# Context keys of a Perceiver layer: turned on VectorE and through DRAM instead of on TensorE; weight sums placed behind the first layer norm

## The chip, the cores and the metric

One core of one Trainium2 chip. The metric is the time of one execution on the device in microseconds (us), median of three runs. All data and all matmuls are float32.

## The reference, cut to what matters

One layer on 256 latent tokens `x` (width 512) with a context of 4096 tokens: cross attention, then a Mamba block, then a mixture of experts, each behind a layer norm. The change is in the attention:

```python
h = layernorm(x)                                    # (256, 512)
q = rope(rms_norm(h @ wq, q_norm_w))                # 16 heads of 128
k = rope(rms_norm(h @ wk, k_norm_w)); v = h @ wv    # 4 key-value heads of 128
kc = rms_norm(ctx @ wk_ctx, k_norm_w)               # context: 4096 keys, no rope
vc = ctx @ wv_ctx
scores = q @ concat(kc, k).T / sqrt(128) + mask     # context open, own tokens causal
out = softmax(scores) @ concat(vc, v) @ wo
x = x + out                                         # then Mamba, then the experts
```

`rms_norm(y, w)` is `y * rsqrt(mean(y*y) + eps) * w`. For a context key this is one factor per key and head, and a weight vector `w` over the 128 channels; the query sees the weights only through the product of the two.

## The kernel before, in words

The program is written with one instruction stream per engine (TensorE is PE, VectorE is DVE, ScalarE is ACT, GpSimd is POOL, SyncE is SP and issues most DMAs). Each engine works through its own stream in order. A scheduler places the instructions of all steps into the streams by their dependencies; semaphore waits follow from the tiles.

**Bounded arm.** A flag computed from the norm weights selects between two arms of the program (L1339). In the arm that runs (`bounded`), no running maximum is kept: the exponent is shifted by a constant.

**Prologue** (L416 to L463). Layer norm of the two token tiles (`layernorm`, L187; its power is a POOL instruction, `power_half`, L181). Then come key and value products of context chunk 0 (`context_pieces`, L273), key, value and query products of the own tokens (`self_block`, L429, ten of these), and for each of the ten a norm and rope in `norm_rope` (L401): ACT copies the product (L404) and squares it (L242), DVE does the rope (L409 to L412) and prepares the power (L184), POOL raises it (`r`, L185) and multiplies (`lacc`, L413), and PE turns the block by four 128x128 transposes (`selfT`, L437).

**Weight sums** (`fast_weights`, L297). The other seven chunks of 512 context tokens use a Strassen-like scheme of seven products for eight. It needs four sums of quarters of `wkv` (the context weights of keys and values in one tile), all on POOL: T1, T2 and T4 (L305 to L307) into weight buffers that come free late in the prologue, and T3 in place (L308). Sums of a context chunk, S1 to S4 (L320 to L323), are POOL's too.

**Attention** (`bounded_attention`, L496). Stage s (0 to 8) scores one chunk of keys: stage 0 the own keys in 12 steps, stage s the context chunk s-1 in 32 steps (4 groups of heads, 2 token tiles, 4 key tiles). A step is a score product (`scT`, L512), an exponential on ACT (L515, its scale `rk` carries the key's norm factor), a running sum on DVE (L523) and, two steps later, a value product (`oT`, L532). From stage 2 on key tiles are taken in the order 1, 3, 2, 0 (`keys_of`, L492).

**Beside the steps** of stages 1 to 7 the next chunk's keys and values are made (`fast_steps`, L310): `extra` is a list of closures, called one by one between the steps at L568. There are 14 products (`ps_kv`, L328), whose results DVE and ACT add up into `kraw` (keys, tokens on partitions) and `v`; after the sixth and the seventh of each half, `key_rms` (L245) squares a key tile for its norm factor. Four `key_transpose` (L265) are among the extras: four PE transposes of 128x128 (`kTp`, L269), then an ACT copy times the key norm weights into `kT` (L270), which lies with channels on partitions. The last two extras load a context chunk and clear a piece of the experts' gather buffer in DRAM.

**Tiles.** `krp` has two buffers of tag `sq`, for the squares. `kvp` has two `kT` and two `v`. `wpool` has six weight buffers; `oacc` and `lacc` are large accumulators, used as scratch in the prologue.

Of the kernel before, what the change touches and what calls it, by code (L numbers as in the profile page):

```python
# [19 lines left out]
P = 128  # L20
# [47 lines left out]
def perceiver_layer(ctx: ExitStack, tc: tile.TileContext, a: dict, out: bass.AP):  # L68
# [17 lines left out]


    load_ctx0 = lambda i, n: nc.sync.dma_start(ctx0[:, i:i + n], a["ctxT"][0, :, i:i + n])
    load_ctx0(0, 1)
    for k in range(0, KD, 2):  # L90
        nc.sync.dma_start(wkc[:, k:k + 2, :], a["wk_ctx"][k * P:(k + 2) * P, :].rearrange("(k p) n -> p k n", p=P))
    nc.sync.dma_start(x_sb, a["x"].rearrange("(t p) d -> p t d", p=P))
    load_ctx0(1, 1)
    load_ctx0(2, 2)
# [21 lines left out]
    xg = tc.dram_tile((ROUNDS * NE * P, DM), FP, name="xg")  # L116
    ye = tc.dram_tile(((NE + 1) * P, DM), FP, name="ye")
    ye2 = tc.dram_tile(((NE + 1) * P, DM), FP, name="ye2")
    sums_d = [tc.dram_tile((SH, P), FP, name=f"sums{t}") for t in range(NT)]

    rope = const.tile([P, NT, 2, HALF], FP, name="rope")
# [7 lines left out]
    def layer(ctx, bounded):  # L129
# [51 lines left out]
        def power_half(dst, src, scale, eps, n):  # L181

            v = small.tile([P, NH], FP, tag="pv", name="pv")
            V.tensor_scalar(v[:, :n], src, scale, eps, ALU.mult, ALU.add)  # L184
            G.tensor_tensor(dst, v[:, :n], mhalf[:, :n], ALU.pow)  # L185

        def layernorm(t):  # L187

            st = small.tile([P, 6], FP, tag="bn", name="bn")
            V.bn_stats(st, x_sb[:, t, :])  # L190
            mv = small.tile([P, 2], FP, tag="mv", name="mv")
            V.bn_aggr(mv, st)
            rs = small.tile([P, 1], FP, tag="rs", name="rs")
            power_half(rs, mv[:, 1:2], 1.0, 1e-5, 1)
            V.tensor_scalar(xn[:, t, :], x_sb[:, t, :], mv[:, 0:1], rs, ALU.subtract, ALU.mult)

        def turn_xn(t, tp):

# [58 lines left out]
        def context_tiles(c):  # L257

            kT = kvp.tile([P, NKV, CK], FP, tag="kT", name="kT")
            v = kvp.tile([P, CK // P, NKV * HD], FP, tag="v", name="v")  # L260
            r = small.tile([P, CK // P, NKV], FP, tag="rk", name="rk", bufs=2)
            kv[c + 1] = (kT, v, r)
            raws = {}

            def key_transpose(i):  # L265
                tp = ps_tp.tile([P, NKV, P], FP, tag="tp", name="kTp")
                raw = raws.pop(i)
                for h in range(NKV):
                    TE.transpose(tp[:, h, :], raw[:, h, :], ident)  # L269
                S.activation(kT[:, :, i * P:(i + 1) * P], tp, AF.Copy, scale=kw_col)  # L270
            return v, r, raws, key_transpose

        def context_pieces(c):  # L273

            ct = ctx_tiles.pop(c)
            v, r, raws, key_transpose = context_tiles(c)

            def key_piece(i):
                ps = ps_mm.tile([P, 512], FP, tag="mm", name="ps_k")
                project(ps, lambda k: ct[:, i, k, :], lambda k: wkc[:, k, :])  # L280
                raws[i] = raw = krp.tile([P, NKV, HD], FP, tag="kraw" if i == 1 else "kn", name="kraw")
                S.copy(raw, ps.rearrange("p (h d) -> p h d", d=HD))
                key_rms(raw, r[:, i, :])

            def value_piece(i):
                ps = ps_mm.tile([P, 512], FP, tag="mm", name="ps_v")
                project(ps, lambda k: ct[:, i, k, :], lambda k: wvc[:, k, :])
                S.copy(v[:, i, :], ps)

            return [[lambda i=i, f=f: f(i) for i in range(CK // P)] for f in (key_piece, value_piece, key_transpose)]  # L290
# [3 lines left out]

        fast = {}

        def fast_weights():  # L297
            fw = [wpool.tile([P, KD, 512], FP, tag="w", name=f"fast{i}") for i in range(3)]
            T = (2, 2, 256)
            fast["T2"], fast["T4"] = carve(fw[0], T, T)  # L300
            fast["S2"], fast["S4"], fast["u3"], fast["u2"] = carve(fw[1], (2, 2, P), (2, 2, P), (2, 256), (2, 256))

            fast["T1"], fast["S1"], fast["S3"] = carve(fw[2], T, (2, 2, P), (2, 2, P))
            b11, b12, b21, b22 = (wkv[:, :, k:k + 2, n:n + 256] for k in (0, 2) for n in (0, 256))
            G.tensor_tensor(fast["T1"], b12, b11, ALU.subtract)  # L305
            G.tensor_tensor(fast["T2"], b22, fast["T1"], ALU.subtract)
            G.tensor_tensor(fast["T4"], b21, fast["T2"], ALU.subtract)  # L307
            G.tensor_tensor(b12, b22, b12, ALU.subtract)  # L308

        def fast_steps(c):  # L310
            ct = ctx_tiles.pop(c)
            v, r, raws, key_transpose = context_tiles(c)
            T1, T2, T4, S1, S2, S3, S4, u3, u2 = (fast[n] for n in ("T1", "T2", "T4", "S1", "S2", "S3", "S4", "u3", "u2"))
            wide = lambda n: (lambda k: wkv[:, :, n % 2 * 2 + k, n // 2 * 256:n // 2 * 256 + 256])
            w11, w21, T3, w22 = (wide(n) for n in range(4))
# [14 lines left out]
            def row(j):  # L330

                m = {}
                bank = lambda: ps_mm.tile([P, 2, 256], FP, tag="mm", name="ps_kv")
                here = lambda i, k0: (lambda k: ct[:, i, k0 + k, :])
                part = lambda s: (lambda k: s[:, j, k, :])

                def put(i, h, ps, more=None):

                    if i not in raws:
                        raws[i] = krp.tile([P, NKV, HD], FP, tag="kraw" if i < 2 else "kn", name="kraw")  # L340
                    to = (raws[i].rearrange("p h d -> p (h d)")[:, h * 256:h * 256 + 256], v[:, i, h * 256:h * 256 + 256])
                    for n in range(2):
                        if more is None:
                            S.copy(to[n], ps[:, n, :])
                        else:
                            V.tensor_tensor(to[n], ps[:, n, :], more[:, n, :], ALU.add)  # L346

                def p1():
                    m["x"] = bank()
                    product(m["x"], here(j, 0), w11)  # L350
                    S.copy(u3, m["x"])

                def p6():
                    m["y"] = bank()
                    product(m["y"], part(S2), by(T2))
                    V.tensor_tensor(u2, m["y"], u3, ALU.add)

                def p2():
                    product(m["x"], here(j, 2), w21, False)
                    put(j, 0, m["x"])  # L360

                def p7():
                    product(m["y"], part(S3), T3, False)
                    V.tensor_tensor(u3, m["y"], u3, ALU.add)

                def p5():
                    m["z"] = bank()
                    product(m["z"], part(S1), by(T1))
                    put(j + 2, 1, m["z"], u3)

                def p4():
                    product(m["y"], here(j + 2, 2), by(T4))
                    put(j + 2, 0, m["y"], u3)
                    key_rms(raws[j + 2], r[:, j + 2, :])

                def p3():
                    product(m["z"], part(S4), w22, False)
                    put(j, 1, m["z"], u2)
                    key_rms(raws[j], r[:, j, :])
                return [p1, p6, p2, p7, p5, p4, p3]  # L380

            turn = lambda i: (lambda: key_transpose(i))
            first, then = row(1), row(0)
            sums()
            return first + then[0:2] + [turn(3)] + then[2:3] + [turn(1)] + then[3:] + [turn(2), turn(0)]


        tab_q, tab_k = carve(oacc, (2, NT, HD), (2, NT, HD))
        room = carve(lacc, *[(REP, HD)] * 8)

        take_ro, take_ru = ring([room[i] for i in (0, 1, 4, 5, 7)]), ring([room[i] for i in (2, 6, 3)])
# [26 lines left out]
        kv[0] = (kT0, v0, None)  # L418
        ctx_k, ctx_v, ctx_t = context_pieces(0)
        for t in range(NT):  # L420
            layernorm(t)
        for i in range(3):
            ctx_k[i]()
        for t in range(NT):
            turn_xn(t, ps_sc.tile([P, 512], FP, tag="sc", name="lnT"))
        rope_table(tab_k, kw_bc)
        rope_table(tab_q, qw_bc)

        def self_block(t, w, tb, dst):  # L429
            ps = ps_mm.tile([P, 512], FP, tag="mm", name="ps_self")  # L430
# [49 lines left out]


        wo = [wpiece(a["wo"][j * 512:(j + 1) * 512, :], f"wo{j}") for j in range(3)]
        fast_weights()
        w_x = []

        def last_weights():
# [9 lines left out]
        def bounded_attention(beside):  # L496
# [50 lines left out]
            for s in range(NC + 1):  # L547
# [4 lines left out]
                    last_weights()  # L552
                extra = []
                if 0 < s < NC:
                    extra = fast_steps(s)
                    if s + 1 < NC:
                        extra.append(lambda: load_ctx(s + 1))
                    extra.append(lambda: clear(s - 1))
                done = 0
                for n, st in enumerate(steps):  # L560
                    if s == 0 and n == 3:
                        for turn in turns:
                            turn()
                    pending.append((*st, scores(*st)))
                    if len(pending) > 2:
                        values(*pending.pop(0))
                    if s < NC:
                        while done < len(extra) * (n + 1) // len(steps):  # L568
                            extra[done]()
                            done += 1  # L570
                    elif n > len(steps) // NT + 1:
# [823 lines left out]
```

## Time and profile before

| | |
|---|---|
| median of 3 runs | 1034.38 us (1034.35 to 1034.86) |
| the profiled execution: its time | 1035.15 us |
| its span, first to last instruction | 1033.4 us |
| granted TensorE clock, mean | 0.997 |
| chain that ended last | PE 91%, POOL 2%, DMA 2%, DVE 2%, ACT 1% of the span |
| prologue, stages 0 to 8, rest | to about 89 us, to about 760 us, to the end |
| `kTp` transposes, L269 | 128, in 32 groups of 4 |
| `kT` copies, L270 | 32, mean 688 ns |

Times in the profile are microseconds from the span's start, or ns where it says "mean ns". A row of groups has line, engine, operation, output and inputs by the program's names, shapes and count; then busy time and mean of one; then the engine's idle time just before, and what ended it. PEld is TensorE's loading of the stationary operand. Each float32 matmul appears as two passes ("x2"). Matmul ends are modelled, since matmuls overlap in a pipeline, so the rate is read from starts: one pass of 128x512 starts 0.43 us after the other.

### The profile page before, as it was taken

The numbers are of one execution on the slowest core, as the hardware profiler recorded it, in microseconds if no ns is written. First come the engines' busy times: TensorE is split into PE (matmuls) and PEld (weight loads), VectorE is DVE, ScalarE is ACT, GpSimd is POOL, SyncE is SP. The second block draws the span as 40 slices with busy tenths as digits, with TensorE's granted clock in tenths as the row PEclk, the third lists the DMA queues.
The fourth block names the chain that finished last, engine by engine and source line by source line (L and its number), as shares of the span: only waits on it lengthen the run. The fifth ranks groups of instructions, "written<-read, shape, count | busy, mean of one in ns | idle before, by whom it ended". The sixth has DMA issues, their size and how long they took to land.

```text
span 1033.4 us, 9074 instructions
## 1 busy us (share of the span) xinstructions
PE 1009.6 (98%) x2930; PEld 492.4 (48%) x2930; DVE 476.7 (46%) x947; ACT 397.1 (38%) x887; POOL 157.2 (15%) x156
## 2 busy tenths in 40 slices
PE   7998999999999999999999999999999999999997
PEld 3443444444444444444444444444556555555553
DVE  2346544344444443443543534466786563322133
ACT  3544344434444534434434434442353531222210
POOL 2374002001001100200200200000023322000022
PEclk9999999999999999999999999999999999999999
DMA  9997001000000100100100000300153457999833
GB/s 336 380 406 273 0 1 41 1 0 22 20 1 1 41 0 1 41 0 1 41 0 1 22 0 1 122 1 0 44 203 122 154 214 285 369 363 360 302 111 97
DMA packets 41499, 113.05 MB, mean 109 GB/s; under 512 B 3777, under 2 KB 4706, under 8 KB 40290
## 3 DMA queue, kind: packets, MB, share of 16 engines
q1 hardware_dynamic: 34336, 96.83, 26.0%
q0 software_dynamic: 2208, 8.39, 2.3%
q10 hardware_dynamic: 4898, 7.16, 1.9%
q8 instruction: 25, 0.41, 0.2%
q14 instruction: 32, 0.26, 0.1%
HBM read 81.42 MB, written 30.95 MB: 109 GB/s over the span
## 4 chain that ended last, share of the span: by engine, by line
PE 91%; POOL 2%; DMA 2%; DVE 2%; ACT 1%; issue 1%; SPq 0%; POOLq 0%; DVEq 0%
PE oT L532 22%; PE scT L512 22%; PE ps_kv L328 16%; PE ps_egu L206 7%; PE ps_self L206 3%; PE ps_ye L1222 2%; PE ps_o L720 2%; PE ps_xbc L206 1%; PE kTp L269 1%; PE ps_ye L1225 1%; PE ps_v L206 1%; DMA yk<-ye,row_y 1%; PE ps_out L910 1%; PE xgTp L1167 1%; PE ps_k L206 1%
## 5 line engine op out<-in xcount | busy, mean ns | idle before, releaser
L523 DVE TENSOR_TENSOR lacc<-lacc,prT 128x512 f32<-128x512 f32 x260 | 183.2, 706 | 263.1 <-ACT prT L515 263.1
L515 ACT ACTIVATE prT<-scT,bq,rk 128x512 f32<-128x512 f32 x256 | 198.3, 775 | 212.9 <-PE scT L512 208.2
L532 PE MATMUL oT<-prT,v 128*128 128x512 f32 x536 | 273.5, 592 | 0.7 <-DVE prT L518 0.7
L512 PE MATMUL scT<-qT,kT 128*128 128x512 f32 x536 | 273.6, 592 | 0.0
L532 PEld LDWEIGHTS oT<-prT,v 128*128 128x128 f32 x536 | 101.7, 190 | 128.8 <-issue 112.4
L512 PEld LDWEIGHTS scT<-qT,kT 128*128 128x128 f32 x536 | 99.0, 190 | 111.2 <-issue 110.9
L185 POOL TENSOR_TENSOR rk<-pv,mhalf 128x4 f32<-128x4 f32 x32 | 32.3, 1010 | 355.5 <-DVE pv L184 354.8
L242 ACT ACTIVATE sq<-kraw 128x128 f32<-128x128 f32 x128 | 38.2, 300 | 90.9 <-DVE kraw L346 90.9
L1182 DVE TENSOR_TENSOR hid<-si,ps_egu 128x128 f32<-128x128 f32 x32 | 9.2, 287 | 94.3 <-ACT si L1180 94.3
L328 PE MATMUL ps_kv<-wkv,fast 128*128 128x512 f32 x112 | 52.6, 592 | 0.0
L328 PE MATMUL ps_kv<-wkv,ctx 128*128 128x512 f32 x112 | 52.6, 592 | 0.0
L538 DVE TENSOR_TENSOR oacc<-oT,oacc 128x512 f32<-128x512 f32 x64 | 43.7, 683 | 1.0 <-PE oT L532 1.0
L1136 POOL DMA_INDIRECT yk<-ye,row_y x12 | 13.2, 1098 | 137.9 <-ACT si L1180 134.6
L328 PEld LDWEIGHTS ps_kv<-wkv,ctx 128*128 128x128 f32 x112 | 21.3, 190 | 26.8 <-issue 25.1
L328 PEld LDWEIGHTS ps_kv<-wkv,fast 128*128 128x128 f32 x112 | 21.3, 190 | 26.8 <-issue 23.9
L1228 ACT COPY y_sb<-ps_ye 128x512 f32<-128x512 f32 x26 | 15.3, 587 | 48.8 <-PE ps_ye L1225 43.0
L1180 ACT ACTIVATE si<-ps_egu 128x192 f32<-128x192 f32 x32 | 10.6, 332 | 58.5 <-PE ps_egu L206 58.5
L346 DVE TENSOR_TENSOR kraw<-ps_kv,fast 128x256 f32<-128x256 f32 x42 | 17.8, 424 | 30.6 <-PE ps_kv L328 30.6
L206 PE MATMUL ps_self<-wq,xT 128*128 128x512 f32 x64 | 30.3, 622 | 0.0
L720 PE MATMUL ps_o<-wo,qT 128*128 128x512 f32 x64 | 28.8, 592 | 0.0
L322 POOL TENSOR_TENSOR fast<-ctx 128x512 f32<-128x512 f32 x7 | 9.3, 1330 | 124.4 <-PE ps_kv L328 124.4
L270 ACT ACTIVATE kT<-kTp,kw_col 128x512 f32<-128x512 f32 x32 | 22.0, 688 | 14.0 <-PE kTp L269 14.0
(293 smaller groups left out, 1191.0 us busy)
## 6 DMA issues: line engine op xcount, KB each, us to landing
xg<-xn SPq DMA_DIRECT2D x6, 2560.0 KB, 21.0
w_in<-in_pairs_dram SPq DMA_DIRECT2D x14, 768.0 KB, 6.4
ctx<-in_ctxT_dram SPq DMA_DIRECT2D x7, 1024.0 KB, 4.9
xg_sb<-xg SPq DMA_DIRECT2D x28, 256.0 KB, 6.5
ye<-y_sb ACTq DMA_DIRECT2D x26, 256.0 KB, 7.0
wkv<-in_pairs_dram SPq DMA_DIRECT2D x6, 768.0 KB, 6.6
w_out<-in_pairs_dram SPq DMA_DIRECT2D x6, 768.0 KB, 6.3
oacc<-in_pairs_dram SPq DMA_DIRECT2D x6, 768.0 KB, 6.3
```

The source lines that it names most:

```text
L185: G.tensor_tensor(dst, v[:, :n], mhalf[:, :n], ALU.pow)
L206: TE.matmul(ps, lhs(k), rhs_of(k), start=(k == 0), stop=(k == KD - 1))
L242: S.activation(sq[:, h, :], raw[:, h, :], AF.Square, accum_out=ss[:, h:h + 1])
L270: S.activation(kT[:, :, i * P:(i + 1) * P], tp, AF.Copy, scale=kw_col)
L328: TE.matmul(ps, lhs(k), rhs(k), start=(start and k == 0), stop=(k == 1), skip_group_check=True)
L512: TE.matmul(sc, kT[:, g, i * P:(i + 1) * P], qT[:, t, heads4(g), :].rearrange("p h q -> p (h q)"), start=True, stop=True)
L515: S.activation(pr, sc, AF.Exp, bias=shift, scale=SCALE if r is None else r[:, i, g:g + 1])
L523: V.tensor_tensor(la, la, pr, ALU.add)
L532: TE.matmul(outs[g, t], v[:, i, g * HD:(g + 1) * HD], pr, start=(n == 0), stop=last)
L538: V.tensor_tensor(ov, outs.pop((g, t)), ov, ALU.add)
L720: TE.matmul(m["ps_o", t], aT[:, t, h, :], wo[j][:, h % 4, :], start=(h == 0), stop=(h == NH - 1))
L1222: TE.matmul(ps[i], h[:, i, :], wd[:, i, :], start=True, stop=False)
```

## The change

In `bounded` alone:

- The four `key_transpose` are no longer among the extras of stages 1 to 7. A new `key_blocks(i)` follows each `key_rms`. One DVE instruction turns each 32x32 block of the 128x512 key tile within its own square and writes the result to `tr` (a buffer of tag `sq`). Four DMAs from SP, one for each 32 partitions, write the blocks to where they belong in a DRAM tile `kd`, in runs of 32 floats (128 bytes, 512 runs in a DMA). A fifth DMA reads the whole back as 128 rows of channels, four runs of 512 bytes each, into `kT`.
- The four key tiles of chunk 0 are still turned on PE. Their copy (L270) no longer multiplies by the key norm weights. Instead each group of queries is multiplied by them on ACT, in place, after its last score of stage 0: eight instructions of 128x512.
- The extras, 14 now, are to be done four steps before the end of a stage. The load of a context chunk and the clearing are called ahead of them.
- T1, T2 and T4 are computed on POOL behind the second layer norm, into `oacc`, and ACT copies them (three of 128x1024) into the weight buffers where they were computed before. T3 and S1 to S4 stay on POOL where they were.
- The first load of `wk_ctx` is three DMAs (quarter, quarter, half) in place of two halves.

```diff
-    for k in range(0, KD, 2):
-        nc.sync.dma_start(wkc[:, k:k + 2, :], a["wk_ctx"][k * P:(k + 2) * P, :].rearrange("(k p) n -> p k n", p=P))
+    load_wkc(0, 1)
+    load_wkc(1, 1)
+    load_wkc(2, 2)
...
+    kd = [tc.dram_tile((CK // P, NKV, HD, P), FP, name=f"kd{c}") for c in range(NC)]
...
-                S.activation(kT[:, :, i * P:(i + 1) * P], tp, AF.Copy, scale=kw_col)
-            return v, r, raws, key_transpose
+                if bounded:
+                    S.copy(kT[:, :, i * P:(i + 1) * P], tp)
+                else:
+                    S.activation(kT[:, :, i * P:(i + 1) * P], tp, AF.Copy, scale=kw_col)
+            def key_blocks(i):
+                tr = krp.tile([P, NKV * HD], FP, tag="sq", name="tr")
+                V.transpose(tr, raws.pop(i).rearrange("p h d -> p (h d)"))
+                for b in range(0, P, 32):
+                    nc.sync.dma_start(kd[c][i, :, :, b:b + 32].rearrange("h (j a) k -> a h j k", a=32),
+                                      tr[b:b + 32, :].rearrange("a (h j k) -> a h j k", h=NKV, k=32))
+                nc.sync.dma_start(kT[:, :, i * P:(i + 1) * P], kd[c][i].rearrange("h d k -> d h k"))
+            return v, r, raws, key_transpose, key_blocks
...
+        def weight_sums(t1, t2, t4):
+            G.tensor_tensor(t1, b12, b11, ALU.subtract)
+            G.tensor_tensor(t2, b22, t1, ALU.subtract)
+            G.tensor_tensor(t4, b21, t2, ALU.subtract)
-        def fast_weights():
+        def fast_weights(sums):
...
-            G.tensor_tensor(fast["T1"], b12, b11, ALU.subtract)
-            G.tensor_tensor(fast["T2"], b22, fast["T1"], ALU.subtract)
-            G.tensor_tensor(fast["T4"], b21, fast["T2"], ALU.subtract)
+            for n, t in zip(("T1", "T2", "T4"), sums):
+                S.copy(fast[n], t)
             G.tensor_tensor(b12, b22, b12, ALU.subtract)
...
                     key_rms(raws[j + 2], r[:, j + 2, :])
+                    if bounded:
+                        key_blocks(j + 2)
...
                     key_rms(raws[j], r[:, j, :])
+                    if bounded:
+                        key_blocks(j)
...
             sums()
+            if bounded:
+                return first + then
             return first + then[0:2] + [turn(3)] + then[2:3] + [turn(1)] + then[3:] + [turn(2), turn(0)]
...
-        tab_q, tab_k = carve(oacc, (2, NT, HD), (2, NT, HD))
+        tab_q, tab_k, *sums = carve(oacc, (2, NT, HD), (2, NT, HD), T, T, T)
...
+        with tc.issue_after(normed.ins):
+            weight_sums(*sums)
...
                 if 0 < s < NC:
+                    if s + 1 < NC:
+                        load_ctx(s + 1)
+                    clear(s - 1)
                     extra = fast_steps(s)
-                    if s + 1 < NC:
-                        extra.append(lambda: load_ctx(s + 1))
-                    extra.append(lambda: clear(s - 1))
...
                     pending.append((*st, scores(*st)))
+                    if s == 0 and st[3] == len(keys_of(s, st[2])) - 1:
+                        q = qT[:, st[2], heads4(st[1]), :]
+                        S.activation(q, q, AF.Copy, scale=kw_col)
...
-                        while done < len(extra) * (n + 1) // len(steps):
+                        while done < min(len(extra), len(extra) * (n + 1) // (len(steps) - 4)):
```

In the streams as they are built, POOL's T1, T2 and T4 stand directly behind the two powers of the layer norm; ahead of them stand nothing but constants, behind them the norm factors of chunk 0's keys. On SP the four writes of the first key tile of a pair come first, then two of the second tile, the read of the first, the other two writes, the read of the second; the load of the next context chunk stands between the two pairs of a stage. The seven clearings of the gather buffer stand in the prologue on SP, in both kernels.

More of the change, by code (lines that the diff above doesn't have):

```diff
@@ L88, in perceiver_layer @@
     load_ctx0 = lambda i, n: nc.sync.dma_start(ctx0[:, i:i + n], a["ctxT"][0, :, i:i + n])
+    load_wkc = lambda k, n: nc.sync.dma_start(wkc[:, k:k + n, :],
+                                              a["wk_ctx"][k * P:(k + n) * P, :].rearrange("(k p) n -> p k n", p=P))
     load_ctx0(0, 1)
-    for k in range(0, KD, 2):
-        nc.sync.dma_start(wkc[:, k:k + 2, :], a["wk_ctx"][k * P:(k + 2) * P, :].rearrange("(k p) n -> p k n", p=P))
+    load_wkc(0, 1)
+    load_wkc(1, 1)
+    load_wkc(2, 2)
     nc.sync.dma_start(x_sb, a["x"].rearrange("(t p) d -> p t d", p=P))
@@ L184, in power_half @@
             V.tensor_scalar(v[:, :n], src, scale, eps, ALU.mult, ALU.add)
-            G.tensor_tensor(dst, v[:, :n], mhalf[:, :n], ALU.pow)
+            return G.tensor_tensor(dst, v[:, :n], mhalf[:, :n], ALU.pow)
         def layernorm(t):
@@ L193, in layernorm @@
             rs = small.tile([P, 1], FP, tag="rs", name="rs")
-            power_half(rs, mv[:, 1:2], 1.0, 1e-5, 1)
+            factor = power_half(rs, mv[:, 1:2], 1.0, 1e-5, 1)
             V.tensor_scalar(xn[:, t, :], x_sb[:, t, :], mv[:, 0:1], rs, ALU.subtract, ALU.mult)
+            return factor
         def turn_xn(t, tp):
@@ L269, in key_transpose @@
                     TE.transpose(tp[:, h, :], raw[:, h, :], ident)
-                S.activation(kT[:, :, i * P:(i + 1) * P], tp, AF.Copy, scale=kw_col)
-            return v, r, raws, key_transpose
+                if bounded:
[10 more added lines that the diff above has]
+            return v, r, raws, key_transpose, key_blocks
         def context_pieces(c):
             ct = ctx_tiles.pop(c)
-            v, r, raws, key_transpose = context_tiles(c)
+            v, r, raws, key_transpose, _ = context_tiles(c)
             def key_piece(i):
@@ L295, in layer @@
         fast = {}
-        def fast_weights():
-            fw = [wpool.tile([P, KD, 512], FP, tag="w", name=f"fast{i}") for i in range(3)]
[L299 to L304, printed above, removed]
-            G.tensor_tensor(fast["T1"], b12, b11, ALU.subtract)
-            G.tensor_tensor(fast["T2"], b22, fast["T1"], ALU.subtract)
-            G.tensor_tensor(fast["T4"], b21, fast["T2"], ALU.subtract)
+        T = (2, 2, 256)
+        b11, b12, b21, b22 = (wkv[:, :, k:k + 2, n:n + 256] for k in (0, 2) for n in (0, 256))
+        def weight_sums(t1, t2, t4):
[3 more added lines that the diff above has]
+        def fast_weights(sums):
+            fw = [wpool.tile([P, KD, 512], FP, tag="w", name=f"fast{i}") for i in range(3)]
+            fast["T1"], fast["T2"] = carve(fw[0], T, T)
+            fast["T4"], fast["S1"], fast["S2"] = carve(fw[1], T, (2, 2, P), (2, 2, P))
+            fast["S3"], fast["S4"], fast["u3"], fast["u2"] = carve(fw[2], (2, 2, P), (2, 2, P), (2, 256), (2, 256))
+            for n, t in zip(("T1", "T2", "T4"), sums):
+                S.copy(fast[n], t)
             G.tensor_tensor(b12, b22, b12, ALU.subtract)
@@ L311, in fast_steps @@
             ct = ctx_tiles.pop(c)
-            v, r, raws, key_transpose = context_tiles(c)
+            v, r, raws, key_transpose, key_blocks = context_tiles(c)
             T1, T2, T4, S1, S2, S3, S4, u3, u2 = (fast[n] for n in ("T1", "T2", "T4", "S1", "S2", "S3", "S4", "u3", "u2"))
@@ L420, in layer @@
         for t in range(NT):
-            layernorm(t)
+            normed = layernorm(t)
         for i in range(3):
@@ L482, in layer @@
         wo = [wpiece(a["wo"][j * 512:(j + 1) * 512, :], f"wo{j}") for j in range(3)]
-        fast_weights()
+        fast_weights(sums)
         w_x = []
```

## The prediction

> **What bounds the kernel now.** First the busy shares (part 1 of the page), then the order of time on TensorE inside the attention, then the chain of work in the prologue, then DVE and the DMAs.
>
> ```profile
> PE 1009.6 (98%) x2930; PEld 492.4 (48%) x2930; DVE 476.7 (46%) x947; ACT 397.1 (38%) x887; POOL 157.2 (15%) x156
> ```
>
> PE is busy nearly everywhere; no other engine reaches half. In the timeline of PE, near the end of stage 1:
>
> ```profile
> 182.25 1.02 PE L532 MATMUL oT<-prT,v 128*128 128x512 f32 x2
> 183.11 0.60 PE L269 MATMUL kTp<-ident,kraw 128*128 128x128 f32 x4
> 183.55 1.02 PE L512 MATMUL scT<-qT,kT 128*128 128x512 f32 x2
> ```
>
> Columns are start and duration; I read starts. A pair of passes takes 0.86 us (183.11 - 182.25), a group of four key transposes 0.44 us (the next group: 185.27 to 185.70, 0.43), with no gap on either side. So in the stages PE is the bound, and a group left out is 0.43 to 0.44 us won. The waits of PE by releaser show only one wait on DVE in stages 0 to 8 (0.7 us, L518), none on DMA.
>
> The prologue is different. The chain that ended last, in order of time, from 69 to 95 us (start, duration, what):
>
> ```profile
> 69.76 1.39 POOL r L185
> ...
> 71.23 1.33 POOL lacc L413
> 72.57 2.31 POOL fast L306
> ...
> 74.96 2.35 POOL fast L307
> 77.31 0.98 POOL r L185
> ...
> 78.36 1.35 POOL lacc L413
> ...
> 79.75 0.66 PE selfT L437 x4
> 80.41 5.15 PE ps_self L206 x8
> ...
> 91.51 1.44 POOL r L185
> ...
> 93.02 1.12 POOL lacc L413
> ...
> 94.19 0.66 PE selfT L437 x4
> ```
>
> POOL is the bound here: T2 and T4 (L306, L307) stand ahead of the next query block's `r` and `lacc`, and PE waits for its transpose (3.0 us before 79.75). The eight passes at 80.41 then take 5.15 us; a like group took 3.45 at 65.23. The granted clock was 0.72 from 80 to 86 us.
>
> What the loss is: from 65.07 to 94.68 us PE starts 48 passes of 0.43 us and four groups of 0.43, 22.4 us of work in 29.6. So 7.2 us are lost.
>
> The DMA issues (us to landing, last column; the third line is from the answer for 751.7 to 753.3 us alone):
>
> ```profile
> ctx<-in_ctxT_dram SPq DMA_DIRECT2D x7, 1024.0 KB, 4.9
> kT<-in_gate_w_dram ACTq DMA_DIRECT2D x1, 64.0 KB, 1.9
> sums<-csT ACTq DMA_DIRECT2D x1, 8.0 KB, 1.4
> ```
>
> The gate weights are what is nearest to the new DMAs: 64 KB in 512 runs of 128 bytes, though a read from DRAM. The 8 KB store shows what landing costs beside the data, 1.4 us. While the gate load ran (2.4 us watched, 528 packets) the 16 DMA engines were busy 17.4%, so the data took 0.42 us.
>
> [...] the trace has 680 to 706 for such rows. No transpose of DVE is in the trace. [...] The trace shows no store in such runs. [...] L411 takes 0.42 us, but 2.58 us at 88.77, where POOL ran L308. [...]
>
> **The change, part by part.** A. *Key transposes leave PE.* 28 of 32 groups (seven chunks of four) by 0.435 us is **12.2 us**, all on the path, as PE is full there. Their 28 copies on ACT (688 ns) go too; ACT is no bound.
>
> B. *DVE turns.* 28 instructions of 128x512. I take 0.69 us by the price above, 19 us in all. [...] DVE is 46% busy in the stages (23.0 of 50 us from 250 to 300) and this adds 2.8 us to some 80 of a stage. Behind it in DVE's stream wait `rk`'s preparation, needed a stage later, and the running sum, whose four `prT` buffers let PE run ahead. Cost 0[...].
>
> C. *The way through DRAM* is off the path as long as key tile 0, the last made and the fourth used, is in `kT` in time. I count from the end of the sixth product (`p4`) of the second half: 174.53 us in the trace. The context load was issued 0.2 us after it and landed at 4.9; the built order has it there again, ahead of both tiles' DMAs. Let c be the data time of one store of 512 runs. Tile 2's four stores then end at 4.7 + 4c, tile 0's four at 4.7 + 8c; 1.4 us to land; the read of 256 KB some 3.5 us with its issue (the ctx piece of 256 KB took 3.6 from issue): 9.6 + 8c, and 0.5 us for SP, which waits in order and can't issue the second half of tile 0's stores before tile 2 has landed: **10.1 + 8c**. Needed: `p4` to `p3` is 5.15 us, and behind `p3` PE has 19 products of 0.86 us to do (8 value, 7 score, two pairs of the next stage) before the score of tile 0: 5.15 + 16.3 = **21.5**. It fits up to c = 1.42. From the gate load 0.42 us is the low bound for c; I take twice that, 0.84[...]: 16.8 us, 4.7 to spare. High bound: all of the gate's 1.9, that is 25.3, 3.8 late in each of seven stages. In stage 7 three weight loads pass the same queue; by the same count its tile 0 needs about 18 of 19 us. Cost 0, with 1.5 once as the upper bound. The buffers: `tr` shares tag `sq` with the squares, yet the built waits are on stores half a stage old. SP's other work (context loads for a stage later) has 80 us of room.
>
> D. *Query scaling*: eight ACT instructions of about 0.69 us in stage 0. ACT has there an exponential of 0.69 per step of 1.72 us. Hidden.
>
> E. *Weight sums.* POOL now waits early for `wv_ctx` (issued 6.4, landed 15.4 us), runs 3 x 2.35 us, is done near 22.5, and its next urgent work is the `r` at 30.3. Hidden; the only cover it could lose is the copies into `xT` (19.1 to 20.4, needed 23.2). In the prologue's end I rebuild the streams: `lacc` of block q21 is ready at 74.9 before PE wants it (75.8); no wait[...]. Block q30's `lacc` ends at 81.5. Then S3, S4, T3, `r`, `lacc` take 8.3 us as before (85.63 to 94.13 with a gap of 0.4), so the last block's transpose starts near 89.8 instead of 94.19: **4.4 us** of the 7.2. POOL stays the bound, which is why not all. Bounds 2.5 (ACT's three copies of 1.05 us delay the squares) and 7.2.
>
> F. *wk_ctx in three loads.* PE may start 1 us sooner, but waits for the second context piece (landed 11.4 us), behind the same bytes. 0; bounds -0.7 (PE had been done there 0.7 us earlier) and +0.45 (one more issue of 0.44 us ahead of it).
>
> Sum: 12.2 + 4.4 = 16.6 us. The profiled execution ran 1035.15 us, span 1033.4; it becomes 1018.6, span 1016.8. The median lies 0.77 lower: 1034.38 - 16.6 = **1017.8 us**.
>
> **The rivals.** *Slow stores (ends slower).* If c is above 1.42 us, PE waits at the fourth score of each stage from 2 to 8, by 10.1 + 8c - 21.5; at 2.37 us a stage, c = 1.71, the whole gain is gone. At c = 2.0: 4.6 x 7 = 32 us, **1050**. For it: [...]no such store in the trace. Against: the gate's 0.42, so it takes a factor of four.
>
> *Only the transposes count.* If POOL's remaining sums and the ACT copies hold the last query blocks as late as now: 1034.4 - 12.2 = **1022.2**. For it: T3, S3, S4 stay, and DVE is slowed by them. Against: T2 and T4 are plainly in the chain.
>
> *No effect.* PE's freed slots become waits for `prT` or a product's bank, because ACT or DVE set the pace of a step: **1034**. Against: ACT waited 208 us for L512's scores.
>
> **Chances.** Forecast (1014.9 to 1021.9: all 7.2 us recovered, or 2.5 with 2 lost) 0.68; transposes only, to 1024 with the same 2 lost, 0.14; slow stores 0.10; a small wait of c between 1.42 and 1.7, some 1028, 0.05; no effect 0.03. The range 1014.9 to 1024 leaves out 0.18. This kernel's measurement tells about 0.2% (2 us) from none: faster 0.68 + 0.14 + 0.05 = 0.87, same 0.03, slower 0.10.
>
> **What would show it.** Right: four `kTp` groups left; in the stages, starts of PE without gaps; `tr` near 0.7 us; landing of the 64 KB stores near 2 to 4 us; no PE wait on `kT<-kd`; `selfT` at about 90 us. Wrong: PE waiting for DMA at the fourth score of a stage (slow stores); PE waiting for DVE; `selfT` still at 94.

## The result, and the profile after

The changed kernel takes **1018.49 us** (1017.85 to 1019.19, five runs) against 1034.62 us for the kernel before in the same comparison: a ratio of 0.9841, 95% interval 0.9828 to 0.9854. Forecast were 1017.8 us and a range of 1014.9 to 1024.0. The profiled execution took 1019.19 us, its span is 1017.4 us: 16.0 us less span than before, where 16.6 were forecast.

The busy shares, from the page:

```profile
PE 996.1 (98%) x2818; PEld 480.9 (47%) x2818; DVE 495.4 (49%) x975; ACT 384.6 (38%) x870; POOL 156.9 (15%) x156
```

PE has 112 instructions fewer: the transposes, 28 groups of four. DVE is 18.7 us busier. The timeline of PE late in stage 1 (start, duration) answers to the one shown of before:

```profile
182.73 1.02 PE L542 MATMUL scT<-qT,kT 128*128 128x512 f32 x2
183.59 1.02 PE L562 MATMUL oT<-prT,v 128*128 128x512 f32 x2
184.45 1.02 PE L542 MATMUL scT<-qT,kT 128*128 128x512 f32 x2
185.31 1.02 PE L562 MATMUL oT<-prT,v 128*128 128x512 f32 x2
```

Pairs start 0.86 us apart, and no transpose stands between them. All that PE waits for, except the waits under 0.7 us, with total, times and longest:

```profile
PE ps_k L211 <- DMA wkv<-in_wk_ctx_dram: 5.4, 1, 5.4
PE ps_out L944 <- DVE qT L938: 1.9, 1, 1.9
PE oT L562 <- DVE prT L548: 1.3, 1, 1.3
PE total L1247 <- DVE hidS L1240: 1.1, 1, 1.1
PE ps_sh L1036 <- DVE sh L1031: 0.9, 1, 0.9
PE ps_dt L211 <- DVE xT L206: 0.8, 1, 0.8
PE ps_pick L1273 <- DVE x_sb L1044: 0.8, 1, 0.8
PE ps_z L211 <- ACT xc L831: 0.7, 1, 0.7
```

No `kT<-kd` is among them: no key comes late. The chain that ended last, at the end of the prologue:

```profile
74.07 1.02 POOL r L189
...
75.17 1.05 POOL lacc L441
...
76.26 0.66 PE selfT L467 x4
76.92 3.45 PE ps_self L211 x8
...
84.60 2.25 DVE pv L188
86.84 0.07 issue
86.91 1.39 POOL r L189
...
88.37 1.12 POOL lacc L441
...
89.54 0.66 PE selfT L467 x4
```

The two `fast` steps are gone from the chain, the eight passes take 3.45 us (5.15 before), and the last `selfT` starts at 89.54 us (94.19). Last, the block transposes and the new transfers (rows of the groups and of the DMA issues; the last column of the latter is us to landing):

```profile
L284 DVE STREAM_TRANSPOSE tr<-kraw 128x512 f32<-128x512 f32 x28 | 19.8, 706 | 0.4
```

```profile
kd<-tr SPq DMA_DIRECT2D x112, 64.0 KB, 2.4
kT<-kd SPq DMA_DIRECT2D x28, 256.0 KB, 2.8
```

### The profile page after: what moved, and what is told of

The parts are those of the page before. It is cut to its first block, busy times and chain, and to the rows that moved or that the text cites. A ratio compares the mean times of both kernels' runs of the same rounds, so it can differ in the third digit from the quotient of the medians.

```text
span 1017.4 us, 9099 instructions
## 1 busy us (share of the span) xinstructions
PE 996.1 (98%) x2818; PEld 480.9 (47%) x2818; DVE 495.4 (49%) x975; ACT 384.6 (38%) x870; POOL 156.9 (15%) x156
## 4 chain that ended last, share of the span: by engine, by line
PE 91%; DMA 2%; DVE 2%; POOL 2%; issue 1%; ACT 1%; SPq 0%; POOLq 0%; DVEq 0%; ACTq 0%
PE oT L562 23%; PE scT L542 22%; PE ps_kv L350 17%; PE ps_egu L211 7%; PE ps_self L211 3%; PE ps_ye L1256 2%; PE ps_o L754 2%; PE ps_ye L1259 1%; PE ps_v L211 1%; PE ps_k L211 1%; PE ps_xbc L211 1%; PE ps_out L944 1%; PE xgTp L1201 1%; PE total L1247 1%; DMA lm<-sums 1%
## 5 line engine op out<-in xcount | busy, mean ns | idle before, releaser
L542 PEld LDWEIGHTS scT<-qT,kT 128*128 128x128 f32 x536 | 101.2, 190 | 124.6 <-issue 123.1
L350 PE MATMUL ps_kv<-fast,fast 128*128 128x512 f32 x112 | 52.6, 592 | 0.0
L350 PEld LDWEIGHTS ps_kv<-fast,fast 128*128 128x128 f32 x112 | 21.3, 190 | 26.8 <-issue 21.8
## 6 DMA issues: line engine op xcount, KB each, us to landing
ctx<-in_ctxT_dram SPq DMA_DIRECT2D x7, 1024.0 KB, 5.0
```

What stands on the lines that cost most here:

```text
L350: TE.matmul(ps, lhs(k), rhs(k), start=(start and k == 0), stop=(k == 1), skip_group_check=True)
L542: TE.matmul(sc, kT[:, g, i * P:(i + 1) * P], qT[:, t, heads4(g), :].rearrange("p h q -> p (h q)"), start=True, stop=True)
```

## The experiments

Medians drift a little from chip to chip (the kernel before took 1034.62, 1035.05, 1034.92 and 1036.23 us in the four comparisons), so each run is read as its ratio to the kernel before on the same chip. Most verdicts rest on distances between three marks in the traces: the first transpose of the layer norm (`lnT`, counted from the span's start), the start of the last `selfT` (counted from `lnT`), and the start of the last sum of `oT` into `oacc` (the end of stage 8, counted from the last `selfT`). The last of these distances is the steadiest: kernels whose stages are built alike agree in it within 0.02 us. The last column is from the second `ps_dt` to `ps_out` behind it, in the Mamba block's second token tile.

| kernel | ratio (95%) | to `lnT` | to last `selfT` | to end of stage 8 | `ps_dt` to `ps_out` |
|---|---|---|---|---|---|
| before | 1 | 18.42 | 75.77 | 671.57 | 25.39 |
| before, again | one run | 18.41 | 74.62 | 671.57 | 25.38 |
| changed | 0.9841 (0.9828 to 0.9854) | 18.52 | 71.02 | 659.28 | 26.61 |
| changed, again | 0.9834 (0.9820 to 0.9847) | 18.10 | 71.02 | 659.28 | 25.84 |
| e1 sums only | 0.9957 (0.9944 to 0.9971) | 19.38 | 71.14 | 671.56 | 25.39 |
| e2 keys only | 0.9892 (0.9876 to 0.9907) | 18.39 | 74.51 | 659.27 | 25.85 |
| e3 spread over all steps | 0.9911 (0.9895 to 0.9927) | 18.78 | 71.02 | 668.26 | 25.37 |
| e4 `tr` four times | 0.9859 (0.9844 to 0.9874) | 18.22 | 71.04 | 660.48 | 26.01 |
| e5 stores three times | 0.9854 (0.9840 to 0.9868) | 18.79 | 71.02 | 661.18 | 25.38 |
| e6 early in stage 7 alone | 0.9851 (0.9835 to 0.9867) | 18.24 | 71.01 | 661.43 | 26.24 |
| e7 early in all but stage 7 | 0.9904 (0.9884 to 0.9923) | 18.27 | 71.01 | 667.12 | 26.47 |
| v1 later S3, S4, T3 | 0.9833 (0.9820 to 0.9845) | 18.74 | 70.53 | 659.23 | 26.03 |
| v2 chunk 0 too | 0.9849 (0.9837 to 0.9862) | 18.51 | 71.26 | 659.27 | 25.79 |
| v3 both | 0.9849 (0.9833 to 0.9864) | 18.28 | 70.75 | 659.22 | 25.37 |

**One part at a time.** e1 is the kernel before with these edits (it also divides the weight buffers as the change does):

```diff
+        with tc.issue_after(normed.ins):
+            weight_sums(*sums)
...
-            G.tensor_tensor(fast["T1"], b12, b11, ALU.subtract)
-            G.tensor_tensor(fast["T2"], b22, fast["T1"], ALU.subtract)
-            G.tensor_tensor(fast["T4"], b21, fast["T2"], ALU.subtract)
+            for n, t in zip(("T1", "T2", "T4"), sums):
+                S.copy(fast[n], t)
```

> The kernel before with the weight sums alone moved as in the change (T1, T2, T4 behind the second layer norm, three ACT copies later; same buffers as in the change). Theory (POOL's queue sets the end of the prologue): the last block's selfT starts at 89.5 instead of 94.2 us, 4.65 us less, 1030.0 us. Rival (only the key transposes count): selfT still near 94, 1034.6. A second rival, that the two parts help each other: 1031 or more.

Measured: 1030.69 us against 1035.05 us, 4.4 us less. The way to the last `selfT` is 71.14 us, the stages are as before. The sums work alone; the first rival is out. So is the second, by the trace: the way is only 0.12 us longer than in the changed kernel. (The `selfT` stood at 90.5, not 89.5, because this execution began 1 us later.)

e2 is the changed kernel with the opposite of that diff.

> The changed kernel with the weight sums back where they were (POOL, late in the prologue); key blocks on DVE and through DRAM, scaled queries, pacing and the three loads stay. Theory: the prologue ends at 94.2 as before, the stages are 28 x 0.439 = 12.3 us shorter, so 1034.6 - 12.3 = 1022.3 us. Rival (a new cost of the DRAM way or of DVE is hidden in the sum): 1024 or more, with the missing time as gaps of PE in stages 1 to 8.

Measured: 1023.62 us, 11.4 us less (ratio 0.9892, 9.6 to 12.8 us). From the last `selfT` to the end of stage 8 it takes 659.27 us, as the whole change does: 12.3 us of the transposes and nothing lost. The parts add: 4.4 + 11.4 = 15.8 us, and the whole change gives 16.1. But the way to `selfT` is 74.51 us, where the kernel before, with the same POOL order, had 75.77. A second profile of each kernel bears on this difference.

> The kernel before, for a second profile. In its first profile PE waited 3.0 us before a selfT at 79.75 us and then ran eight passes at half clock, 1.7 us longer; in the run with the old weight sums and the new keys it waited the same 3.0 us and ran at full clock. If the half clock belongs to the wait, it is there again, and the last selfT is near 94. If it comes and goes, the last selfT is near 92.9 in this profile, and the span 1.3 us shorter.

> The changed kernel again, on the chip of these runs. Theory: 0.984 of the kernel before, as before (1018.5 on its scale), the last selfT at 89.5 and the end of stage 8 at the same distance from it; the piece of the Mamba block that took 1.2 us longer in the first profile (ps_dt to ps_out of the second token tile: 26.6 us against 25.4) is a chance of the DMAs, and lies anywhere between 25.4 and 26.6. Rival (the change lengthens it): 26.6 again.

PE's wait ahead of the piece from 80 to 86 us is this line in both profiles of before (total, times, longest):

```profile
PE selfT L437 <- POOL lacc L413: 3.9, 3, 3.0
```

The piece itself in the stretches of PE (length, PE's busy time and passes, granted clock, DMA share, GB/s), in the first profile of before and then in the second:

```profile
core 0: us, PE busy (x), PEclk, DMA share, GB/s
80.00:86.00 6.00, 6.00 (x14) 0.72 1.05 407
```

```profile
core 0: us, PE busy (x), PEclk, DMA share, GB/s
80.00:86.00 6.00, 6.00 (x18) 1.00 1.05 408
```

Inside the 6 us of the first profile the granted clock was 0.50 from 81 to 84 us. This half clock followed the same wait of 3.0 us once and not the other time (nor in e2, 1.00 in the same 6 us). It comes and goes, and is worth 1.15 us at the last `selfT`. Without it the new order of the sums gives 74.62 - 71.02 = 3.6 us, with it 4.75.

The other executions, timed but not traced, say more on how often. On the three chips of these experiments the kernel before ran 29 times more: 12 times at a mean granted clock of 0.999, taking 1033.4 to 1034.9 us (median 1033.9), and 17 times at 0.995 to 0.998, taking 1034.9 to 1037.7 us (median 1036.0). e1, which differs in the sums alone, ran five times at 0.999 or 1.000; e2, with the old order, ran once at 0.999 (the profiled execution) and three times at 0.996 to 0.998, up to 3.4 us slower. The changed kernel's ten executions, at 0.998 to 1.000, lie within 1.4 us. So a loss of clock goes with the old order and is there more often than not; between the two medians it is about 2 us. Where the clock fell in those executions no trace shows. It is why the medians give e1 4.4 us and not 3.6.

The Mamba piece took 25.84 us in the second profile of the changed kernel, so 26.6 us is not fixed. That it is only a chance is not shown either: the piece took 25.4 us in all three profiles with the old keys, but in only three of the eleven with the new ones, up to 26.61 in the others. It waits there for one transfer of 1 MB (`lm<-sums`): 5.0 to 5.3 us from its issue to its first reader with the old keys, 5.1 to 8.6 us with the new. Whether the change makes that transfer slower stays open. In the first profile the piece cost 1.2 us, more than the 0.6 us that are missing from 16.6.

**Is DVE's share hidden?** e4:

```diff
-                V.transpose(tr, raws.pop(i).rearrange("p h d -> p (h d)"))
+                kr = raws.pop(i).rearrange("p h d -> p (h d)")
+                for _ in range(4):
+                    V.transpose(tr, kr)
```

> The changed kernel with each block transpose on DVE done four times over (2.8 us instead of 0.70 per key tile, 59 us more of DVE in all). Theory (DVE's share is hidden, the four prT buffers let PE run ahead by more than the 2.8 us): no change, 1018.5 within 1. [...] Rival (DVE close to being a bound in the steps): 59 us more, 1075.

Measured: 1020.59 us, about 1.9 us more than the changed kernel by the ratios, whose intervals overlap (the theory had allowed 1); in the traces 1.20 us, all of it in stage 8. DVE did 59 us more (112 instructions, 79.0 us) and in stages 1 to 7 PE lost nothing. The 1.20 us are at the passage from stage 7 to 8. There the changed kernel has three scores in a row behind three value products; in e4 the scheduler put a single score there, and the value product behind it waited 0.9 us for an exponential. That it did so because it counts on later keys is likely, but not shown.

**Are the stores hidden?** e5:

```diff
-                for b in range(0, P, 32):
+                for b in list(range(0, P, 32)) * 3:
```

> The changed kernel with each of the four stores of a key tile issued three times: 12 issues of 0.49 us on SP and 12 x 0.43 us of data per tile (estimates from the changed trace). The last tile then lands about 4 us later, inside the 6.5 us that it has to spare; but the scheduler counts on more and moves products of the next stage ahead of these scores. Theory: keys in time in stages 1 to 6, a small loss at the passage from stage 7 to 8 where no products can be moved ahead: 1019 to 1021. Rival of the prediction (stores in short runs are what PE would wait for): PE waits for kT in each stage, several us each, 1030 or more.

Measured: 1019.86 us; 1.90 us more in the traces, 1.19 of them at the same passage and with the same 0.9 us wait. The other 0.7 us are in stages 2 and 3, where two value products start about 0.35 us late each in an order that was built anew. PE waits for `kT` nowhere. The rival of slow stores is out, even with three times as many.

**What the early end of the extras is worth.** Four steps are 6.9 us, about all the room that the keys have. e3, e6 and e7:

```diff
-                        while done < min(len(extra), len(extra) * (n + 1) // (len(steps) - 4)):
+                        while done < len(extra) * (n + 1) // len(steps):
```

in e3; in e6 the last factor is `(len(steps) - 4 * (s == NC - 1))`, in e7 `(len(steps) - 4 * (s < NC - 1))`.

> The changed kernel with the 14 extras spread over all 32 steps of a stage, not done four steps early. Counted on the changed trace, tile 2 is in kT 5.8 us and tile 0 some 6.5 us before its score; four steps are 6.9 us. Theory with a fixed order: tile 2 is about 1.1 us late in each of seven stages, 1026. But as built the scheduler moves the next stage's products ahead of these scores: behind the last product PE then has about 10.3 us to tile 2 and 16.3 us to tile 0. Then the keys are in time, 1018.5, plus whatever the bunched products cost (their banks must be emptied by DVE and ACT): up to 1 us a stage, 1025. Rival (the DRAM way has plenty of room anyway): 1018.5.

> The changed kernel with the extras done four steps early in stage 7 alone, spread over all steps in stages 1 to 6. Theory (the early end matters where the next stage has no products that could be moved ahead of the scores): the 6.8 us that the spread cost at the passage to stage 8 are not lost, the 1.8 us of the other stages are: 1020.4 if the changed kernel is 1018.5. Rival (it matters in each stage alike): six of seven parts of the 8.6 us are lost, 1026.

> The counterpart: the extras four steps early in stages 1 to 6, spread over all steps in stage 7. Theory: the 6.8 us at the passage to stage 8 are lost, with PE's waits for kT there: 1025.3 if the changed kernel is 1018.5. Rival (it matters in each stage alike): one of seven parts, 1019.7.

Measured: e3 1026.37 us, in the traces 8.98 us more than the changed kernel. e6 1020.58 us, 2.15 us more; e7 1026.11 us, 7.84 us more. The two halves add up to a little over the whole, and about four fifths lie at the one passage from stage 7 to 8. e3's median is near the 1026 of the theory with a fixed order, but by luck: that theory had seven equal losses. In stages 1 to 6 the scheduler moves the next stage's products ahead of the scores whose keys are not there yet, and PE waits for no key; e6 loses 0.36 us in each of stages 2 to 7, at a value product that starts late. Stage 8 makes no more products, so none can be moved ahead of its scores. PE's waits in e7:

```profile
PE scT L542 <- DMA kT<-kd: 3.4, 2, 2.2
...
PE oT L562 <- ACT prT L545: 1.0, 1, 1.0
```

And the chain there:

```profile
656.43 1.73 PE ps_kv L350 x4
...
659.65 0.72 DVE tr L284
...
662.38 2.83 DMA kd<-tr
...
665.29 4.53 DMA kT<-kd
669.82 0.04 issue
669.87 5.49 PE scT L542 x6
```

From the last product's end at 658.16 the key tile takes 11.7 us through sums, squares, block transpose, stores and read. Its read took 4.53 us, not 2.8, with a weight load (`w_in`) in flight, issued 2.4 us before it. Then the six passes took 5.49 us where six of 0.43 take 2.6: behind the waits the clock fell, as the stretches show:

```profile
core 0: us, PE busy (x), PEclk, DMA share, GB/s
...
660.00:668.00 8.00, 5.55 (x12) 1.00 0.77 202
668.00:675.00 7.00, 5.13 (x6) 0.54 0.11 33
```

Of the 7.84 us some 4.3 are waits (3.4 for keys, 1.0 for the exponential behind them) and 2.9 those six passes at the lower clock; the rest is not accounted for. All four executions of e7 ran at a mean clock of 0.995 to 0.997.

**Versions.** v1 takes the last three sums out of the chain, v2 treats chunk 0 as the others, v3 does both.

In v1 `scaled[0]` is POOL's last multiplication in `norm_rope`, and S3 and S4 are wrapped like T3:

```diff
-            G.tensor_tensor(b12, b22, b12, ALU.subtract)
+            with tc.issue_after(scaled[0].ins):
+                G.tensor_tensor(b12, b22, b12, ALU.subtract)
```

In v2 chunk 0's pieces end in `key_blocks`:

```diff
-            return [[lambda i=i, f=f: f(i) for i in range(CK // P)] for f in (key_piece, value_piece, key_transpose)]
+            turn = key_blocks if bounded else key_transpose
+            return [[lambda i=i, f=f: f(i) for i in range(CK // P)] for f in (key_piece, value_piece, turn)]
```

> The changed kernel with S3, S4 and T3 of the first chunk behind the last query block's scaling on POOL (they stood ahead of its two instructions). Theory (POOL's queue is still what holds the last transpose): the scaling can follow DVE at about 84 us, selfT starts near 86 to 87 instead of 89.5, and of the 2.5 us that PE still loses there between 65 and 90 us about 2 are won: 1016.5 if the changed kernel is 1018.5. Rival (DVE sets the pace there, and the three sums now slow its mask products and running sums of stage 0[...]): no gain, 1018.5.

> The changed kernel with chunk 0's four key tiles also turned on DVE and through DRAM: four groups of 0.435 us leave PE in the prologue, four copies leave ACT, DVE gets four of 0.70 us, SP 20 more DMAs beside the weight loads. Theory (PE is full from 19 to 64 us): 1.7 us less, 1016.8. Rival (the end of the prologue is set by the chain over DVE and POOL, and SP's weight loads come later): no gain or a loss, 1018.5 to 1020.

> The changed kernel with both edits: S3, S4 and T3 behind the last scaling, chunk 0's key tiles on DVE and through DRAM. If both theories hold, the gains add: 1018.5 - 2.0 - 1.7 = 1014.8. If one of the rivals holds, the time of the other edit alone.

Measured: 1017.79, 1019.15 and 1018.36 us; none can be told from the changed kernel. v1 won 0.49 us to the last `selfT`, not 2: the rival held. POOL is now done with that block at 85.4 us, but in PE's order a value product stands ahead of its transpose and waits for DVE. PE and then DVE in v1 (start, duration, and in brackets the idle time before and its releaser):

```profile
84.30 2.74 PE L546 MATMUL scT<-qT,kT 128*128 128x512 f32 x6
88.31 1.12 PE L566 MATMUL oT<-prT,v 128*128 128x512 f32 x2 [1.27 <-DVE prT L552]
89.27 0.60 PE L471 MATMUL selfT<-ident,lacc 128*128 128x128 f32 x4
```

```profile
86.08 2.18 DVE L552 TENSOR_TENSOR prT<-prT,upper 128x512 f32<-128x512 f32 x1 [2.67 <-ACT prT L549]
...
90.99 0.68 DVE L552 TENSOR_TENSOR prT<-prT,upper 128x512 f32<-128x512 f32 x1
```

The first mask product takes 2.18 us while POOL forms T3 (from 85.3 to 87.7 us), a later one 0.68. What slows it beside POOL no trace shows. v2 took four transpose groups off PE and won nothing: PE's waits for POOL's `lacc` grew from 0.6 to 2.0 us, two more of them between 39 and 51 us. So in the prologue the chain over ACT, DVE and POOL sets the pace, and time taken from PE came back as waits.

## Why the prediction was right, step by step

The whole: forecast 16.6 us of span, measured 16.0, and 16.1 us between the medians. From the marks of the two first profiles: start -0.10, way to the last `selfT` 4.75, stages 12.29, the rest of the program -0.99. That the sum lies so near is in part luck: the half clock of before (1.15 us) and the slower Mamba piece (1.2 us) happen to cancel in these two profiles. On the chip of the second profiles the medians lie 17.8 us apart (1036.23 and 1018.46). The forecast's upper end of 1021.9 us should be 1021.7 by its own terms (1034.4 - 12.2 - 2.5 + 2).

**A, transposes (12.2).** 12.3 us in the changed kernel, in its repetition and in e2: 0.439 us a group. Right. The rival "only the transposes count" fails on e1, "no effect" on e2.

**B, block transposes (0.69 us, hidden).** One takes 0.706 us. The forecast 0.69 lies among what DVE's products and sums of 128x512 took in the trace of before (mean 680 ns at L544, 706 at L523); that a transpose takes as long was the author's estimate. Hidden: at four times the work stages 1 to 7 (from the last sum into `oacc` of stage 0 to that of stage 7) are 552.63 us in both kernels.

**C, the way through DRAM (hidden).** Right in its outcome, off in its terms. The DMA stretch of the first four stores of stage 1, 5.1 us long (packets, MB, share of 16 engines):

```profile
q1 hardware_dynamic: 2112, 0.26, 33.9%
```

That is 5.1 x 0.339 / 4 = 0.43 us for a store. The prediction took twice the gate load's 0.42, which was its author's estimate. No such doubling shows: the stores in 128-byte runs took 0.43 us, hardly longer than the gate's read in such runs. Longer runs moved faster here: the read back, in runs of 512 bytes, moves 256 KB in 0.88 us (24.5% of 3.6 us watched), twice the rate of the stores. With c = 0.43 the prediction's 10.1 + 8c gives 13.5 us, but the tile was there at about 15.0 us: the stores were not its limit. SP in stage 1:

```profile
179.88 0.83 SPq L286 DMA_DIRECT2D kd<-tr  x2
180.90 0.38 SPq L288 DMA_DIRECT2D kT<-kd  x1
181.32 1.05 SPq L286 DMA_DIRECT2D kd<-tr  x2
184.65 0.38 SPq L288 DMA_DIRECT2D kT<-kd  x1
```

The sixth product ended at 172.43. Tile 0's first store comes 7.4 us later, because the tile must first be made by the seventh product, which ends at 177.58, then summed, squared and turned. The step counted stores queued behind stores and left that out. The read is issued at 184.65 and lands 2.8 us later, 6.4 us ahead of the score at 193.89; the prediction had 4.7 to spare. For stage 7 it had 18 of 19 us; there the read is issued at 658.66, would land near 663.2 by e7's 4.53 us (an estimate), and the score runs at 665.12: about 2 us to spare. What the prediction did not price at all is the part of the change that makes this room. It took the 19 products ahead of the fourth score from the built order and never asked what they would be with the old pacing: with the old pacing 9.0 of the 16 us are lost (e3), and 7.8 hang on the last passage alone (e7).

**D and F (0).** Nothing of the eight scalings is seen: from the first score of stage 0 to that of stage 1 it is 21.42 us in the changed kernel as in the second profile of before. The start wanders between 18.1 and 19.4 us whatever the loads, so that F is nothing or too small to see.

**E, weight sums (4.4).** 4.75 us between the first profiles, in its bounds, and the mechanism held in the main: POOL finished T4 at 22.5 us as forecast, the wait of 3.0 us ahead of the next block shrank to 0.3 (forecast was none, as its `lacc` ended at 76.2 us and not at 74.9), and POOL's last chain ended the prologue at 89.54 (forecast 89.8). That POOL stays the bound, which was to explain why not all is won, holds only in part: with POOL's last sums out of the way (v1) the last `selfT` came 0.49 us earlier, for PE then waits for DVE. And the size rested on one profile with a half clock in it. The order of the sums itself gives 3.6 us; 1.15 us came from a stall whose after-effect is there in some executions only, so that 4.4 lies near 4.75 partly by luck.

The prediction counted the slow passes of before into its loss of 7.2 us as if they came with the wait each time. In the middle of this kernel they did not: behind the same wait of 3.0 us the half clock came in one of three profiles (before 0.72 over the 6 us; before again and e2 1.00). What decides it no run shows.

## What to carry to other kernels

Where TensorE was full, what was moved off it was worth its starts exactly (28 x 0.44 us), but only in the stages where it was really that engine that was full: in the prologue the same move was worth nothing (v2). A long way round through DRAM, 15.0 us in stage 1, cost nothing where its length was covered by work ordered ahead of its reader, and 7.84 us where at one passage it was not (e7), so ask at each passage, the last one above all, what could be run in the meantime. Before a gain is read from a stall in one profile, look at more executions, their clocks too: part of the stall may be there in some of them only.

## What the runs showed of the hardware

Stores of 64 KB in 128-byte runs to DRAM moved at the rate of a read in such runs, 0.43 us (changed) against 0.42 (the gate load of before). A half clock behind a 3.0 us wait of TensorE came once in three profiles (granted clock 0.72 in before against 1.00 in before again and e2, in the same 6 us), and the mean clock was 0.995 to 0.998 in 17 of 29 further executions of the kernel before, 0.999 in the others. In e7, behind waits of 3.4 us for keys (two, the longest 2.2) and 1.0 us for an exponential, the granted clock was 0.54 from 668 to 675 us. A VectorE product of 128x512 took 2.18 us while a GpSimd sum ran, and a later one 0.68 (v1).
